# Three products instead of four in a spectral layer, and column terms read from a column-ordered copy

## The chip, the cores and the metric

The kernel runs on one core of a Trainium2 chip. The metric is device time in microseconds (us), the median of several runs. The core has a matrix engine (TensorE, PE in the profile, with its weight loads shown apart as PEld), a vector engine (VectorE, DVE), an activation engine (ScalarE, ACT), GpSimd (POOL) and a queue that issues the transfers (SyncE, SP). Each takes its instructions in order and waits for the others by semaphores. Matrix products are written to PSUM, in eight banks; everything else lies in SBUF.

## The reference

An image of 48 x 48 tokens with 768 channels goes through a transformer block and then through a spectral layer. Shortened to what matters here:

```python
# layer 0: attention with decomposed relative positions, 12 heads of 64 channels
q, k, v = heads(layernorm(x) @ qkv_w + qkv_b)
attn = einsum('bqc,bkc->bqk', q * scale, k)
rel_h = einsum('bhwc,hkc->bhwk', q.reshape(nh, 48, 48, hd), rel_pos_h[coords])
rel_w = einsum('bhwc,wkc->bhwk', q.reshape(nh, 48, 48, hd), rel_pos_w[coords])
attn = softmax(attn + rel_h[..., :, None] + rel_w[..., None, :])
x = x + (attn @ v) @ proj_w + proj_b
x = x + gelu(layernorm(x) @ mlp_w1 + mlp_b1) @ mlp_w2 + mlp_b2
# layer 1: spectral layer, 8 blocks of 96 channels
xr, xi = rfft2(x)
o1r = relu(xr @ w1[0] - xi @ w1[1] + b1[0])
o1i = relu(xi @ w1[0] + xr @ w1[1] + b1[1])
o2r = softshrink(o1r @ w2[0] - o1i @ w2[1] + b2[0], 0.01)
o2i = softshrink(o1i @ w2[0] + o1r @ w2[1] + b2[1], 0.01)
y = irfft2(o2r + 1j * o2i) + x
```

All data are float32. The first spectral layer is a complex product, written with four real products per block of 96 channels.

## The kernel before

**Stages.** The kernel normalises the tokens and makes queries, keys and values (written to DRAM by pairs of heads), then runs attention pair after pair, then the projection, the MLP in three passes over 768 tokens (projection aside, the large products are done by a scheme with seven products of half size in place of eight), and last the spectral layer: a Fourier transform along the rows, written to DRAM and read back by frequency, the work along the columns, and the way back. A general path behind a test on the data is not taken.

**Attention.** There are six pairs of heads (`pr`), six chunks of 384 queries (`c`) and two halves of the 2304 keys (`u`); one *run* is one (pr, c, u), with nine key tiles of 128. A run first makes the nine score tiles. For each, `scores` issues two products q·k (L552) and two that add the position terms (L558) into one of three PSUM buffers `sp`, and ScalarE takes the exponential out of it (L562). VectorE adds the exponentials up (L619). Then come the products of the run before with the values (`products`, L567), in groups, and between the groups small pieces of work. After the second half of a chunk `set_aside` copies the finished output out of PSUM on ScalarE (L575); `finish` sums the denominators (L582), reads them on ScalarE (L587) and divides.

**Position terms.** `columns(pr, i)` makes the column terms of eight image columns: for each column w and each head of the pair one product of 48 queries against 48 positions (L262). The queries lie in `qT` in the order (chunk of 8 image rows, block of 16 image columns, row, column), so the 48 queries of one image column are read from `qT` 16 elements (64 bytes) apart. `relative(pr, c)` does the same for the image rows of one chunk (L284); its 48 queries are three groups of 16 neighbours. Both write into one PSUM bank (`small_bank`, a single one during attention), and `two_parts` takes it out with two ScalarE copies (L233 and L234) and one VectorE subtraction (L235). The terms of pair pr + 1 are made during pair pr: the six `columns` in the runs (3,1), (4,0) and (4,1), two in each, and the first `relative` in (5,0) and (5,1). `fetch` brings the next pair's queries and keys in at run (1,0). For pair 0 this happens in the stage before. The column terms are kept in `col_parts`, from which transfers on the SP queue (L297, L301) build the tiles `terms` that L558 reads.

**Spectral stage.** One `Unit` is a half of the channels (four blocks of 96) and up to four of the 25 kept frequencies; there are 14 units, 12 with four frequencies (192 columns per block) and 2 with one (48 columns). In each round four steps i are taken, and in each step, in this order: `back(i)` of the unit three rounds older (L1240), `second(i)` of the one two rounds older (L1221), `first(i)` of the one a round older (L1197, L1198) and `columns(i)` of the newest (L1178). `first(i)` does all frequencies of block i: four products into one PSUM tile `lp`, then real part with bias and relu on VectorE (L1199), imaginary part on ScalarE (L1203), and the negated imaginary part on GpSimd (L1207), all into `o1`. `second(i)` does all four blocks of frequency i and so needs the outputs of all four `first` of its unit; it uses `o1` as the weights. `balanced_copy` takes `columns` and `back` out of PSUM, on VectorE for even i (L77) and ScalarE for odd i (L75). Rounds near the end also hold pieces of `rows_back` (L1261), the transform back along the rows with the last addition.

**Order.** PE's order is that of the text throughout; SP's is too, up to the end of attention. The other queues are ordered by a scheduler at build time, except where the text says otherwise. Matrix products of float32 appear as two PE instructions (two passes) in the profile.

Of the kernel before, what the change touches and what calls it, by code (L numbers as in the profile page):

```python
# [9 lines left out]
F32 = mybir.dt.float32  # L10
# [34 lines left out]
def block_then_afno(  # L45
# [143 lines left out]
    with ExitStack() as flag_scope:  # L189
# [11 lines left out]
        with ExitStack() as att:  # L201
# [18 lines left out]
            def small_bank():  # L220
                banks.append(banks.pop(0))
                return banks[-1]
# [16 lines left out]
            def fetch_values(pr):  # L239
                nc.sync.dma_start(  # L240
                    out=heads[pr][2], in_=v_d[:, ts(pr, P)].rearrange("(k p) f -> p k f", p=P)
                )

            def fetch(pr, pool=None):
# [7 lines left out]
                nc.sync.dma_start(out=kT, in_=k_d[pr])  # L252
                heads[pr] = qT, kT, v.rearrange("p (k f) -> p k f", k=NT)

            def columns(pr, i):

                qT = heads[pr][0].rearrange("p (c b h w) -> p b w c h", c=6, b=3, h=8)
                ps = small_bank().rearrange("p (w c h) -> p w c h", w=8, h=8)
                for r in range(8):
                    w = 8 * i + r  # L260
                    for j in range(2):
                        nc.tensor.matmul(  # L262
                            ps[ds(64 * j, HW), r], relT[:, j, 1, 47 - w : 95 - w],
                            qT[:, w // 16, w % 16], start=True, stop=True,
                        )
                hi, lo = (
                    a.rearrange("p (c b h w) -> p b w c h", c=6, b=3, h=8)[
                        :, i // 2, ds(8 * (i % 2), 8)
                    ]
                    for a in (col_hi, col_lo)  # L270
                )
                two_parts(hi, lo, ps)
# [260 lines left out]
            with tc.manual_schedule(engines={mybir.EngineType.PE, mybir.EngineType.SP}):  # L533
# [4 lines left out]
                small_banks(psum, 1)  # L538
                kv_b = att.enter_context(tc.tile_pool(name="att_kv_b", bufs=1))
                o_pool = att.enter_context(tc.tile_pool(name="att_o", bufs=2))  # L540
                kv = [None, kv_b]
                exps = main.rearrange("p (n j q) -> p n j q", n=18, j=2)
                RUN = 9

                def scores(pr, c, kt, p):

                    qT, kT = heads[pr][:2]
                    a, b = divmod(kt, 3)
                    sp = psum.tile([P, 2, 512], F32, name="sp", bufs=3)
                    for j in range(2):  # L550
                        at = slice(64 * j, 64 * j + 64)
                        nc.tensor.matmul(  # L552
                            sp[:, j, :G], kT[at, ts(kt, P)], qT[at, ts(c, G)],
                            start=True, stop=False,
                        )
                    for j in range(2):
                        at = slice(64 * j, 64 * j + 64)
                        nc.tensor.matmul(  # L558
                            sp[:, j, :G], select[at, a % 2], ready[pr, c][at, a // 2, b],
                            start=False, stop=True,  # L560
                        )
                    nc.scalar.activation(p, sp[:, :, :G], AF.Exp, scale=HD**-0.5)  # L562

                def products(op, v, kt0, ps, first):
                    for i in range(first, first + 3):
# [35 lines left out]

                runs = [(pr, c, u) for pr in range(NC) for c in range(T // G) for u in range(2)]
                waiting = done = op = acc = None
                for n, (pr, c, u) in enumerate(runs):
                    if (c, u) == (1, 0) and pr < NC - 1:
                        fetch(pr + 1, kv[(pr + 1) % 2])
                    if (c, u) == (2, 0) and pr < NC - 1:
                        fetch_values(pr + 1)
                    if (c, u) == (4, 0) and pr == NC - 1:
                        nc.sync.dma_start(out=pw, in_=proj_w.rearrange("(c p) f -> p c f", p=P))  # L610
                    if u == 0:
                        acc = o_pool.tile([P, 2, G], F32, name="acc")
                    made = []
                    for i in range(RUN):
                        kt = RUN * u + i
                        p = exps[:, (RUN * n + i) % 18]
                        scores(pr, c, kt, p)
                        if kt:
                            nc.vector.tensor_tensor(acc, made[0] if kt == 1 else acc, p, ALU.add)  # L619
                        made.append(p)  # L620
                    small = []
                    if u and c < 3:
                        small.append(partial(relative, pr, c + 3))
                    if pr < NC - 1:
                        if (c, u) in ((3, 1), (4, 0), (4, 1)):
                            i = 2 * (2 * (c - 3) + u - 1)
                            small += [partial(columns, pr + 1, i), partial(columns, pr + 1, i + 1)]
                        if (c, u) == (5, 0):
                            small += [partial(relative, pr + 1, 0), partial(relative, pr + 1, 1)]
                        if (c, u) == (5, 1):  # L630
                            small.append(partial(relative, pr + 1, 2))
                    if u and done:
                        small.insert(1, partial(finish, *done))
                    for i in range(3):
                        if waiting and i:
                            products(*waiting, 3 * (i - 1))
                        if i < len(small):
                            small[i]()
                    if waiting:
                        products(*waiting, 6)  # L640
                        if u == 0:
                            done = (*runs[n - 1][:2], done_acc, set_aside(waiting[0]))
                    if u == 0:
                        op = psum.tile([P, G], F32, name="op")
                    else:
                        done_acc = acc
                    waiting = (op, heads[pr][2], RUN * u, made)
                for i in (0, 3, 6):
                    products(*waiting, i)
                finish(*runs[-1][:2], acc, set_aside(waiting[0]))  # L650
# [457 lines left out]
    with ExitStack() as sp:  # L1108
# [20 lines left out]
        a1 = view(BS, 2, NB, BS)  # L1129
        a2 = view(BS, NB, 2, BS)  # L1130
        d2 = view(2 * HW, NB, BS)
        a1n = view(BS, NB, BS)
        irows = view(4 * KW, 6, P)
        icols = view(2 * HW, 2 * HW)
        cols = view(2 * HW, 2 * HW)
# [9 lines left out]
            )  # L1145
        nc.sync.dma_start(out=icols, in_=c_icols)
        nc.sync.dma_start(out=irows, in_=c_irows)
        nc.vector.tensor_scalar(a1n, a1[:, 1], -1.0, None, ALU.mult)

        z2_h = [z.rearrange("(r k) c -> r k c", k=KW) for z in z2]  # L1150
        NBH = NB // 2
# [4 lines left out]
        class Unit:  # L1156
# [27 lines left out]
            def first(self, i):  # L1184

                if i == 0:

                    self.o1 = mid.tile([BS, NBH, 4, 3, HW], F32, name="o1")
                b = NBH * self.half + i
                re, im = (  # L1190
                    self.xf[:, i, t, : self.nk, :].rearrange("p k h -> p (k h)") for t in range(2)
                )
                lp = psum.tile([BS, 2, 4 * HW], F32, name="lp", tag="l")
                for t, (wr, wi) in enumerate(
                    ((a1[:, 0, b], a1n[:, b]), (a1[:, 1, b], a1[:, 0, b]))
                ):
                    nc.tensor.matmul(lp[:, t, : self.n], wr, re, start=True, stop=False)  # L1197
                    nc.tensor.matmul(lp[:, t, : self.n], wi, im, start=False, stop=True)  # L1198
                nc.vector.tensor_scalar(  # L1199
                    self.o1[:, i, : self.nk, 1], by_k(lp[:, 0, : self.n]), d1[:, 0, b : b + 1], 0.0,  # L1200
                    ALU.add, ALU.max,
                )
                nc.scalar.activation(  # L1203
                    self.o1[:, i, : self.nk, 2], by_k(lp[:, 1, : self.n]), AF.Relu,
                    bias=d1[:, 1, b : b + 1],
                )
                nc.gpsimd.tensor_scalar(  # L1207
                    self.o1[:, i, : self.nk, 0], self.o1[:, i, : self.nk, 2], -1.0, None, ALU.mult
                )
# [22 lines left out]
            def back(self, i):  # L1232

                if i >= self.nk:
                    return
                zz = self.zz[i]
                if i % 2 == 0:
                    self.y = mid.tile([2 * HW, 2, CH], F32, name="y", bufs=3)
                yp = psum.tile([2 * HW, CH], F32, name="yp", tag="y")
                nc.tensor.matmul(  # L1240
                    yp, icols, zz.rearrange("p n o -> p (n o)"), start=True, stop=True
                )
                balanced_copy(i, self.y[:, i % 2, :], yp)
                if i % 2 or i == self.nk - 1:
                    n = i % 2 + 1
                    nc.sync.dma_start(
                        out=z2_h[self.half][:, ds(self.k0 + i + 1 - n, n), :], in_=self.y[:, :n]
                    )
# [169 lines left out]
```

## Time and profile before

The median of 3 runs is 2955.97 us (2951.86 to 2956.34). The profiled execution took 2962.34 us, of which 2960.5 us are the span of its instructions.

| stretch of the profiled execution | us | PE busy | ACT busy | DVE busy | POOL busy |
|---|---|---|---|---|---|
| 533 to 1495, most of attention | 962.0 | 962.0 | 562.4 | 707.8 | 43.0 |
| 1650 to 2696, MLP and rows forward | 1046.0 | 1037.0 | 149.2 | 675.1 | 330.4 |
| 2696 to 2916, the spectral units | 220.0 | 218.8 | 43.3 | 101.7 | 84.8 |
| 2916 to the end, rows back | 44.5 | 35.4 | 0.0 | 14.0 | 0.0 |

Busy times are sums of the stretches in which an engine has an instruction under way. A matrix product is pipelined: the next starts before it ends, so the distance between two starts says more of PE than the duration of one.

### The profile page before, as it was taken

Reading aid. Unit: us, or ns where it says so; the run is one execution under the profiler, and the core shown is the slowest. Engines: PE = TensorE matmul, PEld = TensorE weight load, DVE = VectorE, ACT = ScalarE, POOL = GpSimd, SP = SyncE. Lnnn points to the kernel's source line nnn. Section 1 sums busy time; section 2 is a strip of 40 time slices with the busy share of each in tenths; the row PEclk is TensorE's granted clock in tenths of the full one; section 3 lists DMA queues with packets and bytes.
Section 4 is the critical chain, followed back from the end, with each engine's and each line's share of the span. In section 5 each row is a group of like instructions: output and inputs, shape, how many; then the busy total and the mean of one; then the engine's idle time right before and its main releaser. Section 6 shows DMA issues by size and latency. Waiting matters only on the chain. (4 is left out here: it accounts for less than half of the span.)

```text
span 2960.5 us, 40962 instructions
## 1 busy us (share of the span) xinstructions
PE 2902.6 (98%) x15771; PEld 1762.2 (60%) x15771; DVE 1768.2 (60%) x2548; ACT 881.1 (30%) x1372; POOL 610.2 (21%) x564
## 2 busy tenths in 40 slices
PE   6999999999999999999999999999999999999998
PEld 4555655555556555555555555555555555557995
DVE  4342327777777777777633666675666566665443
ACT  1011125555556555565500210122011211111210
POOL 2302110000000000000043223342332323322441
PEclk9999999999999999999999999999999999999999
DMA  3423275173461725535252111112111211213225
GB/s 119 150 83 123 88 163 123 26 135 64 75 132 33 139 42 97 113 50 89 59 177 75 42 54 54 64 62 68 54 64 60 75 49 64 64 57 93 83 83 174
DMA packets 202817, 253.03 MB, mean 85 GB/s; under 512 B 21618, under 2 KB 180978, under 8 KB 201078
## 3 DMA queue, kind: packets, MB, share of 16 engines
q1 hardware_dynamic: 202614, 250.32, 33.2%
q8 instruction: 127, 2.08, 0.3%
q14 instruction: 76, 0.62, 0.1%
HBM read 136.40 MB, written 50.14 MB: 63 GB/s over the span
## 5 line engine op out<-in xcount | busy, mean ns | idle before, releaser
L619 DVE TENSOR_TENSOR acc<-acc,main 128x768 f32<-128x768 f32 x576 | 551.9, 958 | 202.0 <-ACT main L562 145.4
L562 ACT ACTIVATE main<-sp 128x768 f32<-128x768 f32 x648 | 522.1, 811 | 155.8 <-PE sp L558 148.6
L558 PE MATMUL sp<-terms,select 64*128 64x384 f32 x1296 | 413.1, 630 | 0.0
L1032 DVE TENSOR_TENSOR main<-o,main 128x384 f32<-128x384 f32 x540 | 299.4, 556 | 41.0 <-PE o L1030 2.1
L970 PE MATMUL h<-shared,w 128*128 128x384 f32 x864 | 296.6, 486 | 0.8 <-issue 0.8
L552 PE MATMUL sp<-shared 64*128 64x384 f32 x1296 | 267.9, 490 | 2.2 <-DVE o L452 2.2
L552 PE MATMUL sp<-qT,kT 64*128 64x384 f32 x1296 | 266.5, 487 | 0.0
L597 POOL TENSOR_TENSOR inverse<-inverse,rden 128x384 f32<-128x384 f32 x36 | 46.3, 1287 | 1031.6 <-DVE rden L594 961.6
L441 PE MATMUL m<-main 128*128 128x384 f32 x756 | 248.4, 490 | 6.2 <-DVE main L172 2.9
L970 PEld LDWEIGHTS h<-shared,w 128*128 128x128 f32 x864 | 164.4, 190 | 116.1 <-issue 2.2
L970 PE MATMUL h<-shared,w1s 128*128 128x384 f32 x648 | 226.6, 486 | 0.0
L567 PE MATMUL op<-main,shared 128*64 128x384 f32 x1296 | 221.3, 488 | 0.0
L567 PE MATMUL op<-main,v 128*64 128x384 f32 x1296 | 219.9, 488 | 0.0
L441 PEld LDWEIGHTS m<-main 128*128 128x128 f32 x756 | 143.4, 191 | 108.7 <-issue 10.1
L976 ACT ACTIVATE hT<-c,vec 128x384 f32<-128x384 f32 x108 | 66.4, 615 | 466.1 <-DVE c L982 466.0
L982 DVE TENSOR_TENSOR c<-h,u 128x384 f32<-128x384 f32 x108 | 60.2, 557 | 212.4 <-PE h L970 212.4
L1030 PE MATMUL o<-w,hT 128*128 128x384 f32 x432 | 175.2, 487 | 3.7 <-DVE mv L118 2.0
L1030 PE MATMUL o<-w2s,hs 128*128 128x384 f32 x432 | 174.9, 487 | 1.4 <-DVE hs L155 1.3
L558 PEld LDWEIGHTS sp<-terms,select 64*128 64x128 f32 x1296 | 125.6, 187 | 84.1 <-issue 0.5
L970 PEld LDWEIGHTS h<-shared,w1s 128*128 128x128 f32 x648 | 123.1, 190 | 85.9
L154 POOL TENSOR_TENSOR w1s<-w 128x384 f32<-128x384 f32 x36 | 36.2, 1006 | 612.5 <-PE o L1030 420.8
L552 PEld LDWEIGHTS sp<-shared 64*128 64x128 f32 x1296 | 117.7, 187 | 60.3 <-issue 23.1
(150 smaller groups left out, 3892.3 us busy)
## 6 DMA issues: line engine op xcount, KB each, us to landing
w<-in_mlp_w_dram SPq DMA_DIRECT2D x72, 768.0 KB
terms<-col_parts SPq DMA_DIRECT2D x432, 72.0 KB
terms<-row_hi SPq DMA_DIRECT2D x216, 72.0 KB
terms<-row_lo SPq DMA_DIRECT2D x216, 72.0 KB
main<-in_qkv_w_dram SPq DMA_DIRECT2D x36, 384.0 KB
z<-zt SPq DMA_DIRECT2D x48, 150.0 KB
zo<-z SPq DMA_DIRECT2D x12, 600.0 KB
x<-in_x_dram SPq DMA_DIRECT2D x18, 384.0 KB
```

The source lines that it names most:

```text
L441: nc.tensor.matmul(bank, a[:, c, :], b[:, c, :], start=(first and c == 0), stop=(c == 2), skip_group_check=not first,)
L552: nc.tensor.matmul(sp[:, j, :G], kT[at, ts(kt, P)], qT[at, ts(c, G)], start=True, stop=False,)
L558: nc.tensor.matmul(sp[:, j, :G], select[at, a % 2], ready[pr, c][at, a // 2, b], start=False, stop=True,)
L562: nc.scalar.activation(p, sp[:, :, :G], AF.Exp, scale=HD**-0.5)
L567: nc.tensor.matmul(op[ts(j, 64)], v[:, kt0 + i, ts(j, 64)], ps[i][:, j, :], start=(kt0 + i == 0), stop=(kt0 + i == NT - 1),)
L597: nc.gpsimd.tensor_tensor(inverse, inverse, rden, ALU.add)
L619: nc.vector.tensor_tensor(acc, made[0] if kt == 1 else acc, p, ALU.add)
L970: nc.tensor.matmul(bank[i], a[:, c, :], b[:, c, :], start=(start and c == 0), stop=(c == 2), skip_group_check=not start,)
L976: nc.scalar.activation(h[:, i, ts(k, G)], src, AF.Gelu, bias=col(V_B1 + 2 * n + i))
L982: nc.vector.tensor_tensor(t, src, other, ALU.add)
L1030: nc.tensor.matmul(bank[k], a, b, start=start, stop=True, skip_group_check=not start)
L1032: nc.vector.tensor_tensor(dst, bank[k], dst, ALU.add)
```

## The change

There are three parts.

1. `first(i)` uses three products per block instead of four. With re, im the two parts and w0, w1 the weights, it makes l1 = (re + im)·w0, then re·(w1 - w0) and im·(-w1 - w0); the real part is l1 plus the third, the imaginary part l1 plus the second. VectorE makes re + im (`both`), ScalarE copies l1 out of PSUM (`p_both`), VectorE adds it to both products at once (`pre`), and both relus are done on ScalarE. The PSUM tile l1 has one buffer; the tile `yp` of `back` goes from two buffers to one. Two weight tables `a1d` and `a1e` are made by three VectorE operations in place of one.
2. For the pairs 1 to 5, `columns` reads `by_column`, in which the 48 queries of a column are neighbours. ScalarE makes it with 30 copies of 128 x 384 (`in_columns`), two at the end of each of the runs (2,1), (3,0) and (3,1).
3. During attention ScalarE's order is that of the text.

```diff
@@ columns
+                bank = small_bank()
+                ps = bank.rearrange("p (w c h) -> p w c h", w=8, h=8)
                 for r in range(8):
                     w = 8 * i + r
                     for j in range(2):
                         nc.tensor.matmul(
-                            ps[ds(64 * j, HW), r], relT[:, j, 1, 47 - w : 95 - w],
-                            qT[:, w // 16, w % 16], start=True, stop=True,
+                            bank[ds(64 * j, HW), ts(r, HW)] if pr else ps[ds(64 * j, HW), r],
+                            relT[:, j, 1, 47 - w : 95 - w],
+                            by_column[:, w] if pr else qT[:, w // 16, w % 16],
+                            start=True, stop=True,
                         )
@@ attention
+                by_column = o_pool.tile([P, HW, HW], F32, name="by_column", bufs=1)
...
+                def in_columns(pr, i):
+
+                    q = heads[pr][0].rearrange("p (c b h w) -> p b w c h", c=6, b=3, h=8)
+                    nc.scalar.copy(
+                        by_column[:, ts(i, 8)].rearrange("p w (c h) -> p w c h", c=6),
+                        q[:, i // 2, ds(8 * (i % 2), 8)],
+                    )
...
+                with tc.manual_schedule(engines={mybir.EngineType.Activation}):
                     for n, (pr, c, u) in enumerate(runs):
...
                         if waiting:
                             products(*waiting, 6)
                             if u == 0:
                                 done = (*runs[n - 1][:2], done_acc, set_aside(waiting[0]))
+                        if pr < NC - 1 and (c, u) in ((2, 1), (3, 0), (3, 1)):
+                            for i in range(2):
+                                in_columns(pr + 1, 2 * (2 * (c - 2) + u - 1) + i)
@@ spectral stage
-        a1n = view(BS, NB, BS)
+        a1d = view(BS, NB, BS)
+        a1e = view(BS, NB, BS)
...
-        nc.vector.tensor_scalar(a1n, a1[:, 1], -1.0, None, ALU.mult)
+        nc.vector.tensor_tensor(a1d, a1[:, 1], a1[:, 0], ALU.subtract)
+        nc.vector.tensor_scalar(a1e, a1[:, 1], -1.0, None, ALU.mult)
+        nc.vector.tensor_tensor(a1e, a1e, a1[:, 0], ALU.subtract)
@@ first
+                both = mid.tile([BS, 4 * HW], F32, name="both", bufs=3)
+                nc.vector.tensor_tensor(both[:, : self.n], re, im, ALU.add)
+                l1 = psum.tile([BS, 4 * HW], F32, name="l1", tag="l1", bufs=1)
                 lp = psum.tile([BS, 2, 4 * HW], F32, name="lp", tag="l")
-                for t, (wr, wi) in enumerate(
-                    ((a1[:, 0, b], a1n[:, b]), (a1[:, 1, b], a1[:, 0, b]))
-                ):
-                    nc.tensor.matmul(lp[:, t, : self.n], wr, re, start=True, stop=False)
-                    nc.tensor.matmul(lp[:, t, : self.n], wi, im, start=False, stop=True)
-                nc.vector.tensor_scalar(
-                    self.o1[:, i, : self.nk, 1], by_k(lp[:, 0, : self.n]), d1[:, 0, b : b + 1], 0.0,
-                    ALU.add, ALU.max,
+                nc.tensor.matmul(lp[:, 0, : self.n], a1e[:, b], im, start=True, stop=True)
+                nc.tensor.matmul(lp[:, 1, : self.n], a1d[:, b], re, start=True, stop=True)
+                nc.tensor.matmul(
+                    l1[:, : self.n], a1[:, 0, b], both[:, : self.n], start=True, stop=True
                 )
-                nc.scalar.activation(
-                    self.o1[:, i, : self.nk, 2], by_k(lp[:, 1, : self.n]), AF.Relu,
-                    bias=d1[:, 1, b : b + 1],
+                p = mid.tile([BS, 4 * HW], F32, name="p_both", bufs=3)
+                nc.scalar.copy(p[:, : self.n], l1[:, : self.n])
+                pre = mid.tile([BS, 2, 4 * HW], F32, name="pre", bufs=2)
+                nc.vector.tensor_tensor(
+                    pre[:, :, : self.n], lp[:, :, : self.n],
+                    p[:, : self.n].unsqueeze(1).to_broadcast([BS, 2, self.n]), ALU.add,
                 )
+                for t in range(2):
+                    nc.scalar.activation(
+                        self.o1[:, i, : self.nk, 1 + t], by_k(pre[:, t, : self.n]), AF.Relu,
+                        bias=d1[:, t, b : b + 1],
+                    )
...
-                yp = psum.tile([2 * HW, CH], F32, name="yp", tag="y")
+                yp = psum.tile([2 * HW, CH], F32, name="yp", tag="y", bufs=1)
```

The order of the instructions otherwise: PE, SP and GpSimd issue the same as before but for the products named and the place of four small loads for the spectral weights. On ScalarE the attention part differs by the 30 copies alone, and in the spectral part `xf` of odd steps now stands between the copy of l1 and the two relus of the same step. On VectorE the last `pre` of a round is followed by the first `both` of the next, then the copy of `yp`, then two more `both`.

More of the change, by code (lines that the diff above doesn't have):

```diff
@@ L253, in fetch @@
                 heads[pr] = qT, kT, v.rearrange("p (k f) -> p k f", k=NT)
+            by_column = None
             def columns(pr, i):
                 qT = heads[pr][0].rearrange("p (c b h w) -> p b w c h", c=6, b=3, h=8)
-                ps = small_bank().rearrange("p (w c h) -> p w c h", w=8, h=8)
+                bank = small_bank()
+                ps = bank.rearrange("p (w c h) -> p w c h", w=8, h=8)
                 for r in range(8):
@@ L603, in block_then_afno @@
                 waiting = done = op = acc = None
[L604 to L640, printed above, removed]
-                        if u == 0:
[L642 to L647, printed above, removed]
@@ new lines, in block_then_afno @@
+                with tc.manual_schedule(engines={mybir.EngineType.Activation}):
+                    for n, (pr, c, u) in enumerate(runs):
+                        if (c, u) == (1, 0) and pr < NC - 1:
+                            fetch(pr + 1, kv[(pr + 1) % 2])
+                        if (c, u) == (2, 0) and pr < NC - 1:
+                            fetch_values(pr + 1)
+                        if (c, u) == (4, 0) and pr == NC - 1:
+                            nc.sync.dma_start(out=pw, in_=proj_w.rearrange("(c p) f -> p c f", p=P))
+                        if u == 0:
+                            acc = o_pool.tile([P, 2, G], F32, name="acc")
+                        made = []
+                        for i in range(RUN):
+                            kt = RUN * u + i
+                            p = exps[:, (RUN * n + i) % 18]
+                            scores(pr, c, kt, p)
+                            if kt:
+                                nc.vector.tensor_tensor(acc, made[0] if kt == 1 else acc, p, ALU.add)
+                            made.append(p)
+                        small = []
+                        if u and c < 3:
+                            small.append(partial(relative, pr, c + 3))
+                        if pr < NC - 1:
+                            if (c, u) in ((3, 1), (4, 0), (4, 1)):
+                                i = 2 * (2 * (c - 3) + u - 1)
+                                small += [partial(columns, pr + 1, i), partial(columns, pr + 1, i + 1)]
+                            if (c, u) == (5, 0):
+                                small += [partial(relative, pr + 1, 0), partial(relative, pr + 1, 1)]
+                            if (c, u) == (5, 1):
+                                small.append(partial(relative, pr + 1, 2))
+                        if u and done:
+                            small.insert(1, partial(finish, *done))
+                        for i in range(3):
+                            if waiting and i:
+                                products(*waiting, 3 * (i - 1))
+                            if i < len(small):
+                                small[i]()
+                        if waiting:
+                            products(*waiting, 6)
+                            if u == 0:
+                                done = (*runs[n - 1][:2], done_acc, set_aside(waiting[0]))
+                        if pr < NC - 1 and (c, u) in ((2, 1), (3, 0), (3, 1)):
+                            for i in range(2):
+                                in_columns(pr + 1, 2 * (2 * (c - 2) + u - 1) + i)
+                        if u == 0:
+                            op = psum.tile([P, G], F32, name="op")
+                        else:
+                            done_acc = acc
+                        waiting = (op, heads[pr][2], RUN * u, made)
```

## The prediction

> **What bounds the kernel now.** I read the page first, then the busy time by stretches, then the timeline in the two places that the change touches.
>
> ```profile
> span 2960.5 us, 40962 instructions
> PE 2902.6 (98%) x15771; PEld 1762.2 (60%) x15771; DVE 1768.2 (60%) x2548; ACT 881.1 (30%) x1372; POOL 610.2 (21%) x564
> ```
>
> By stretches (the window, its length, busy time of PE, PEld, DVE, ACT and POOL, the granted clock, the DMA share, GB/s):
>
> ```profile
> 533.00:1495.00 962.00, 962.00 (x7891) 555.75 (x7888) 707.80 (x707) 562.37 (x797) 42.99 (x34) 1.00 0.43 83
> 2696.00:2916.00 220.00, 218.75 (x1798) 195.65 (x1798) 101.73 (x220) 43.26 (x105) 84.83 (x106) 1.00 0.32 94
> ```
>
> TensorE has work in all of attention and in all but 1.3 us of the spectral units. So TensorE time saved there is time saved, until another engine's answer is late. Two questions follow: how much TensorE work goes, and which answer is late next.
>
> The timeline around a block of column terms (L262) and one of row terms (L284):
>
> ```profile
> 1108.47 1.55 PE L262 MATMUL small<-shared,relT 128*48 128x48 f32 x32
> 1109.84 2.12 PE L567 MATMUL op<-main,v 128*64 128x384 f32 x12
> ...
> 1040.99 0.93 PE L284 MATMUL small<-qT,relT 128*48 128x48 f32 x32
> 1041.75 2.12 PE L567 MATMUL op<-main,v 128*64 128x384 f32 x12
> ```
>
> Both blocks are 32 passes over 48 columns with equal weights. From first start to the next group's start the column terms take 1.37 us, the row terms 0.76. What differs is how the moving operand is read: 64 bytes apart, or in runs of 16 neighbours.
>
> ScalarE at the end of run (3,0) of one pair (set_aside, then the next run's exponentials), with the fourth score tile's start:
>
> ```profile
> 883.24 0.48 ACT L575 COPY ot<-op 128x384 f32<-128x384 f32 x1 [5.15 <-PE op L567]
> 884.25 6.55 ACT L562 ACTIVATE main<-sp 128x768 f32<-128x768 f32 x8 [0.54 <-PE sp L558]
> 885.68 0.81 PE L552 MATMUL sp<-shared 64*128 64x384 f32 x4
> ```
>
> Eight exponentials take 6.55 us, 0.82 each, and a score tile also takes 0.82 on TensorE: ScalarE can't catch up within a run. The first exponential ends at 885.07, and the fourth tile, which reuses its buffer, starts at 885.68: some 0.6 us of room.
>
> The end of a unit's last `first` and the start of the next round:
>
> ```profile
> 2736.96 0.49 PE L1198 MATMUL lp<-xf,shared 96*96 96x192 f32 x2
> 2737.28 0.84 PE L1178 MATMUL fp<-shared,zi 96*96 96x96 f32 x8
> 2737.48 0.41 DVE L1199 TENSOR_SCALAR o<-lp,d 96x192 f32<-96x192 f32 x1 [0.29 <-PE lp L1198]
> 2737.93 0.42 ACT L1203 ACTIVATE o<-lp,d 96x192 f32<-96x192 f32 x1 [2.63 <-DVE o L1199]
> 2737.96 0.81 PE L1240 MATMUL yp<-zz,shared 96*96 96x384 f32 x2
> 2738.25 0.46 ACT L75 COPY xf<-fp 96x384 f32<-96x384 f32 x1
> 2738.43 0.69 POOL L1207 TENSOR_SCALAR o<-o 96x192 f32<-96x192 f32 x1 [0.16 <-ACT o L1203]
> 2738.61 1.52 PE L1221 MATMUL mp<-shared,o 96*96 96x96 f32 x16
> ```
>
> This is the one tight loop: product, VectorE, ScalarE, GpSimd, and back to TensorE, which uses the result as weights in `second`. GpSimd ends at 2739.12. The 16 passes of `second` start 0.085 apart; the last block's first pass is the 13th (2739.63), and the pass that needs GpSimd's result is the 15th (2739.80). Between the last `first` and that pass lie the other work of the round, `columns` 0.68 and `back` 0.65. So 0.68 us of room today.
>
> **Column terms, gain.** 30 of the 36 blocks change (pairs 1 to 5). The new operand is fully contiguous, so the row terms' price applies: 30 x (1.37 - 0.76) = 18.3 us. Bounds: nothing, if the reading is not the cause; and some 20, if 48 neighbours go slightly better than three groups of 16.
>
> **Column terms, cost.** ScalarE gets 30 copies. No row shows ScalarE reading SBUF with such a stride. Near rows: PSUM to SBUF without stride 0.48 (L575), the cast that writes `col_parts` in this same stride 0.84. I take 0.84, the row with the like stride, 0.48 as the lower end.
>
> ```profile
> L234 ACT CAST col_parts<-small 128x384 fp32r<-128x384 f32 x36 | 30.0, 833 | 0.0
> L234 ACT CAST row_hi<-small 128x384 fp32r<-128x384 f32 x36 | 17.5, 485 | 0.0
> ```
>
> The Trainium skill, "SBUF — State Buffer", in its note on cachelines under Door 1, says that SBUF has lines of 16 bytes and that each access into a new line pays a penalty. By it both the old products and the new copies pay, which agrees with the 1.37 against 0.76 above; no run here shows a strided read by ScalarE alone, and the page would make me take the upper end, as the L234 rows do. With 0.48 a copy the sum at the end would be 27.6 us, by the page 23.9 or less.
>
> Two copies (1.68) stand at the end of three runs. At (2,1) and (3,1) ScalarE idles 4.28 and 1.72 us before the next exponentials (the timeline at 870.74 and 901.15), which covers them; the queries were asked for at 830.5, three runs earlier. At (3,0) program order puts them behind set_aside, which waits for the last value product, so the 5.15 us of idle time ahead of it does not help: exponentials start at 883.72 + 1.68 = 885.40, the first ends at 886.22, 0.54 after TensorE wants its buffer. ScalarE then stays late through the run, and the single bank of the first column block comes free about 0.2 late for `finish`. 0.74 x 5 pairs = 3.7 us; at 0.48 a copy it is nothing. If the idle cover at (3,1) went too, another 5 x 1 or so.
>
> **Spectral layer, gain.** In the timeline the eight passes of a full `first` start at 2735.98 and `columns` follows at 2737.28: 1.30 us, 0.1625 a pass. Two passes less: 0.325 x 48 = 15.6 us. The eight short ones take 0.64, so 0.16 x 8 = 1.3. Sum 16.9.
>
> **Spectral layer, cost.** Count from the end of the last `first` pass (2737.45 = 0), signals of 0.04 to 0.08 as above. Copy of l1: 0.04 to 0.45 (0.41 as for 96x192 rows). `pre`, 96x384 with PSUM input, 0.55 (L1225): 0.49 to 1.04. In ScalarE's new order xf stands ahead of the relus; `columns` frees it at 0.80, and it ends at 1.26. Two relus of 0.42: 2.10. GpSimd 0.69 from 2.18: 2.87. Needed at 2.35, less some 0.13 for the weight load ahead of it (2738.61 shows PEld one step before PE): 2.22. TensorE waits 0.65 us, once per unit, not per block, since the other three blocks have a round. Eight units are of this kind: 5.2. The first unit has no `back` in between (deadline 0.65 earlier: 1.3), the sixth no `columns` and no xf (1.1). The two short units and the two among the last rounds have 0.45 to 2.0 us of room today and other work in between; I put none on them. Sum 7.6. Lower bound 2: relus overlapping as L233 and L234 do (0.38 from start to start at 0.48) and a copy at 0.30. Upper bound 16.9, GpSimd slowed.
>
> For that last: VectorE's first and second `both` of the next round (two SBUF inputs) fall beside GpSimd's negation, and the rows of L157 show operations of that kind stretching, VectorE from 546 to 1346 ns and GpSimd from 993 to 1322, where both run at once. The same page, under "Who interferes with whom", has a VectorE operation with two SBUF inputs and a GpSimd operation lock each other out whole. It would add at most one `both` (an estimate of 0.35 from the page's rule and the 0.41 row) to ten waits, 3.5 us, and the sum would be 20.4. Without the page the rows of L157 alone put the upper bound there.
>
> **At no cost.** Two more VectorE operations on the weight tables, 0.55 each, fall before 2662, where VectorE idles 3.31 us at 2659.34; without that cover 1.1 us. The single `yp` is copied out within 1.5 us of its product and wanted again after 3.66. VectorE per step goes from about 1.86 to 2.35 of 3.66 us. The four moved loads go out with the same neighbours.
>
> **Sum.** 18.3 - 3.7 + 16.9 - 7.6 = 23.9 us. Against its own execution 2960.5 - 23.9 = 2936.6 of span; that execution (2962.34) stands 6.4 above the median, so 2955.97 - 23.9 = 2932.
>
> **Rivals.**
> - *Spectral gain handed back.* Room 0.68 us, chain longer by 1.2 at least; with GpSimd and xf both late, 1.2 to 1.5 us a unit takes the 16.9. Against: the round has 14.6 us, only its seam is tight. Time 2955.97 - 14.6 = 2941.
> - *Both costs hidden.* Copies at 0.48 and overlapping relus: 18.3 + 16.9 - 2 = 33, time 2923.
> - *The copy changes nothing on TensorE*, the stride not being the cause, so that 1.37 stays. Against: no other difference between the two blocks. 16.9 - 7.6 - 3.7: time 2950.
> - *Slower: ScalarE becomes the bound of attention.* Place: the six copies per pair ahead of exponentials that can't catch up. If one takes d, (3,0) loses 2d - 1.1, (3,1) 2d - 2.3, (2,1) 2d - 4.8. At d = 3 us: 4.9 + 3.7 + 1.2 = 9.8 a pair, 49 in all, against gains of 18.3 + 9.3: time 2977. It decides from about d = 2.5. Against: the strided row is 0.84.
>
> **How the numbers follow.** The forecast as summed, 2925 to 2938: 0.59. Gain handed back (2938 to 2946): 0.18. Both hidden (2918 to 2925): 0.08. Copy without effect (2946 to 2956): 0.09. Slower: 0.06. Time 2932; range 2919 to 2946, which leaves out the last two and the lower edge, 0.17. About 0.2%, 5.9 us, is what a measurement of this kernel can tell from no change. Of the copy-without-effect case 0.03 ends below 2950, the rest within the bound, and so does 0.01 of the handed-back case: faster 0.59 + 0.17 + 0.08 + 0.03 = 0.87, same 0.07, slower 0.06.
>
> **What would show it.** L262 of pairs 1 to 5 at some 0.76 us a block; the copies' mean between 480 and 850 ns; TensorE idle or a wider start distance at the first score tiles of (3,1) and nowhere else in attention; in the spectral units six passes in 0.98 us a step, and in `second` one late pass per round, ended by GpSimd, of about 0.65. The prediction is wrong if L262 stays at 1.37, if ScalarE's copies are beyond 1 us, or if TensorE waits within every step.

## The result, and the profile after

The changed kernel takes 2927.09 us (median of 4 runs, 2923.02 to 2934.48), the kernel before in the same comparison 2955.19: 0.9911 of it, 95% interval 0.9899 to 0.9923, some 28 us less. In a second comparison the ratio was 0.9910 (0.9891 to 0.9929). The forecast was 2932.

The head of the page after:

```profile
span 2922.9 us, 40961 instructions
PE 2864.6 (98%) x15659; PEld 1724.2 (59%) x15659; DVE 1791.0 (61%) x2606; ACT 936.3 (32%) x1514; POOL 609.8 (21%) x564
```

TensorE has 112 instructions less and is as full as before; ScalarE has 55 us more work. The span is 37.6 us shorter than that of the execution before, more than the medians tell. To see why, the profiled executions of the kernels are cut below at the starts of events that each has, read from the timelines: the first score product, the last product with the values, the first product of the first spectral layer, the last of the second layer, and the end of the span.

| us | before | after | spectral only | columns only | no program order | copies early | relus swapped | repaired |
|---|---|---|---|---|---|---|---|---|
| up to attention | 431.8 | 425.9 | 432.7 | 427.2 | 427.1 | 426.6 | 429.3 | 429.6 |
| attention | 1062.5 | 1045.6 | 1062.5 | 1045.6 | 1057.7 | 1043.7 | 1045.7 | 1043.8 |
| projection, MLP, rows forward | 1206.2 | 1204.4 | 1205.4 | 1207.0 | 1205.2 | 1205.7 | 1203.2 | 1203.6 |
| spectral units | 208.8 | 198.6 | 198.6 | 208.8 | 198.6 | 198.6 | 193.9 | 192.8 |
| rest | 51.2 | 48.3 | 50.0 | 50.0 | 49.0 | 50.8 | 47.1 | 53.0 |
| span | 2960.5 | 2922.9 | 2949.2 | 2938.6 | 2937.6 | 2925.4 | 2919.2 | 2922.8 |

Attention and the spectral units repeat to 0.05 us in kernels that share that part. The first, third and fifth row vary by 4 to 7 us between kernels that are the same there, or differ there only by the weight tables and one wait, both under 1 us (see below); the rest is the spread of the runs. So the change is worth 16.9 us in attention and 10.2 in the spectral units; what the two spans differ in beyond these 27.1 lies in the rows that vary.

**Attention after.** The end of run (3,0) in the timeline, as shown of before, and the first column block:

```profile
870.53 0.48 ACT L590 COPY ot<-op 128x384 f32<-128x384 f32 x1 [5.15 <-PE op L582]
870.90 1.59 ACT L574 COPY by_column<-qT 128x384 f32<-128x384 f32 x2
872.39 6.91 ACT L569 ACTIVATE main<-sp 128x768 f32<-128x768 f32 x9
873.26 0.30 PEld L559 LDWEIGHTS sp<-shared 64*128 64x128 f32 x4 [0.59 <-ACT main L569]
...
878.38 0.93 PE L265 MATMUL small<-by_column,relT 128*48 128x48 f32 x32
879.14 1.15 PE L582 MATMUL op<-main,shared 128*64 128x384 f32 x6
```

The block takes 0.76 us from start to start, where it took 1.37. The two copies stand between set_aside and the exponentials, and the fourth score tile waits for the first exponential. That score phase takes 7.97 us where all others after the first take 7.58: 0.39 us, in each of five pairs, and nothing else in attention is later.

**The spectral seam after.** From the last `first` of a unit to the second layer of the next round:

```profile
2710.11 0.49 PE L1223 MATMUL l<-both,shared 96*96 96x192 f32 x2
2710.44 0.84 PE L1202 MATMUL fp<-shared,zi 96*96 96x96 f32 x8
2710.64 0.32 ACT L1227 COPY p_both<-l 96x192 f32<-96x192 f32 x1 [1.56 <-PE l L1223]
2710.99 0.55 DVE L1229 TENSOR_TENSOR pre<-lp,p_both 96x384 f32<-96x384 f32 x1 [0.31 <-ACT p_both L1227]
2711.32 0.47 ACT L75 COPY xf<-fp 96x384 f32<-96x384 f32 x1 [0.36 <-PE fp L1202]
2711.69 0.80 ACT L1234 ACTIVATE o<-pre,d 96x192 f32<-96x192 f32 x2
2711.76 1.35 PE L1252 MATMUL mp<-shared,o 96*96 96x96 f32 x14
...
2712.57 0.76 DVE L1218 TENSOR_TENSOR both<-xf 96x192 f32<-96x192 f32 x2
2712.58 0.88 POOL L1238 TENSOR_SCALAR o<-o 96x192 f32<-96x192 f32 x1 [0.82 <-ACT o L1234]
2713.51 0.41 PE L1252 MATMUL mp<-shared,o 96*96 96x96 f32 x2 [0.40 <-POOL o L1238]
```

Read it as a chain: l1, copy, addition, xf, two relus, negation, and TensorE stops after the 14th pass of `second` until GpSimd is done. From the 14th start (2712.87) to the 15th (2713.51) it is 0.64 us instead of 0.085. GpSimd's negation takes 0.88 where it took 0.69, beside two `both` on VectorE. The loss of such a unit, counted over the 15th and the 16th start against steps of 0.085, is 0.64 as well. The first unit loses 1.1 us in all and the sixth 1.0, as they lack other work in the round; all the waits of the second layer come to 7.0 us (0.2 in the kernel before).

### The profile page after: what moved, and what is told of

Its sections match the earlier page's. It is cut to its first block, busy times and chain, and to the rows that moved or that the text cites. A ratio compares the mean times of both kernels' runs of the same rounds, so it can differ in the third digit from the quotient of the medians.

```text
span 2922.9 us, 40961 instructions
## 1 busy us (share of the span) xinstructions
PE 2864.6 (98%) x15659; PEld 1724.2 (59%) x15659; DVE 1791.0 (61%) x2606; ACT 936.3 (32%) x1514; POOL 609.8 (21%) x564
```

## The experiments

**Each part by itself.** Two kernels: the kernel before with one part of the diff each.

```diff
 (spectral only: the kernel before up to the spectral stage, the changed one from there)
-        a1n = view(BS, NB, BS)
+        a1d = view(BS, NB, BS)
+        a1e = view(BS, NB, BS)
...
```

> The kernel before with the spectral part of the change alone (three products, one yp buffer, two weight tables). Theory (each part is worth its TensorE time less the waits it makes): from the first product of the first layer to the last product of the second some 10.2 us shorter than before, as in the changed kernel, with one wait of 0.64 us per unit in the second layer; attention unchanged at 7.58 us of scores per run and 1.35 us per column block; the whole about 9 to 11 us below before. Rival (the parts help each other, or what the changed kernel gained outside attention and the spectral stage belongs to this part): clearly more than 12 or less than 7 us.

Measured: 2941.19 us against 2955.35, ratio 0.9952 (0.9938 to 0.9966); units 198.6 us as in the changed kernel, attention 1062.5 as before, waits of 0.64 per unit. The median moved 14 us, beyond the 12 allowed, so the times alone do not refute the rival: their interval reaches from 10 to 18 us. The trace does for this stage, where the part is worth 10.2, as in the changed kernel.

```diff
 (columns only: the changed kernel up to the spectral stage, the kernel before from there)
+                by_column = o_pool.tile([P, HW, HW], F32, name="by_column", bufs=1)
...
+                            in_columns(pr + 1, 2 * (2 * (c - 2) + u - 1) + i)
...
```

> The kernel before with the column part alone (copies on ScalarE, contiguous reads, ScalarE in program order during attention). Theory: attention 16.9 us shorter (5 x 3.76 less 5 x 0.39), spectral stage as before; the whole about 15 to 19 us below before. Rival (a good part of the 28 us came from something that neither part owns, such as the transfers before attention): below 13 or above 22 us.

Measured: 2938.95, ratio 0.9942 (0.9925 to 0.9959); attention 1045.6, units 208.8. In the traces the parts are independent: each stage is as long as in the changed kernel, 27.1 us less in the two together. The medians of the parts add to 30.6 us, the whole is 28.1 below before, which is the same within the spread.

**Is the program order on ScalarE needed?** The same changed kernel, without it:

```diff
-                with tc.manual_schedule(engines={mybir.EngineType.Activation}):
-                    for n, (pr, c, u) in enumerate(runs):
+                for n, (pr, c, u) in enumerate(runs):
```

> The changed kernel without the fixed program order on ScalarE: the scheduler now places the six copies of a pair in one run, between exponentials. Theory (ScalarE keeps no more than TensorE's pace in the score phase, 0.82 us a tile for both, so a copy among exponentials is paid beyond some 0.6 us of buffer room): six copies of 0.85 are 5.1 us, so one score phase per pair grows from 7.58 to about 12 us; five pairs lose 20 to 23 us, which takes the whole column gain and leaves the kernel at 2945 to 2952 us. Rival (the fixed order is only a matter of form, the copies hide wherever they stand): within 3 us of the changed kernel.

Measured: 2940.63, ratio 0.9947 (0.9931 to 0.9964), and attention at 1057.7. ScalarE's timeline in one pair:

```profile
683.51 3.25 ACT L569 ACTIVATE main<-sp 128x768 f32<-128x768 f32 x4 [4.28 <-PE sp L565]
686.65 2.37 ACT L574 COPY by_column<-shared 128x384 f32<-128x384 f32 x3
688.90 0.83 ACT L569 ACTIVATE main<-sp 128x768 f32<-128x768 f32 x1
689.61 1.63 ACT L574 COPY by_column<-shared 128x384 f32<-128x384 f32 x2
691.11 0.84 ACT L569 ACTIVATE main<-sp 128x768 f32<-128x768 f32 x1
691.81 0.88 ACT L574 COPY by_column<-shared 128x384 f32<-128x384 f32 x1
692.56 2.23 ACT L569 ACTIVATE main<-sp 128x768 f32<-128x768 f32 x3
```

All six copies stand among the exponentials of one score phase. That phase takes 10.65 us instead of 7.58 in three pairs and 11.47 in a fourth. In the remaining pair the copies begin after the sixth exponential instead of the fourth, TensorE finishes its score tiles into the three buffers, and the phase stays at 7.58. The clock tells the fourth pair from the three: around its copies the mean clock is 0.72, in the same place of another pair 1.00 (the last three figures of a row are clock, DMA share and GB/s).

```profile
690.00:696.00 6.00, 4.88 (x32) 2.15 (x32) 4.04 (x5) 4.79 (x7) 0.00 (x0) 1.00 0.75 120
1047.00:1053.00 6.00, 4.88 (x21) 2.12 (x22) 3.83 (x4) 3.92 (x6) 0.00 (x0) 0.72 0.71 123
```

Against the changed kernel attention loses 12.1 us. The sign was as expected; the loss is half of the 20 to 23 us, and the kernel is faster than the 2945 to 2952 that were forecast. Three things make it smaller. Nine exponentials without copies take 7.35 us and these end after 11.28, so six copies add 3.9 us and not 5.1, since each begins before the one ahead of it has ended; with the room in the buffers TensorE loses 3.1 a pair. One pair of five loses nothing. And the 0.39 of run (3,0) is gone in all five pairs, 1.95 us. About 1.6 us of the 12.1 goes with the low clock in the fourth pair (its run is 18.25 us long, those of the three others 16.6). The rival falls: with 12.1 of 16.9 us, most of the column gain hangs on where the copies stand.

**What makes a column block slow?** The products read the queries at a distance of 1, 2, 3, 4 and 16 elements, one distance per pair:

```diff
-                            by_column[:, w] if pr else qT[:, w // 16, w % 16],
+                            heads[pr][0][:, bass.DynSlice(8 * w, HW, step=STEP[pr])] if pr
+                            else qT[:, w // 16, w % 16],
```

> The changed kernel, but the column products of pair 1, 2, 3, 4, 5 read 48 elements of the queries at a distance of 1, 2, 3, 4, 16 elements (4, 8, 12, 16, 64 bytes) instead of the column-ordered copy; the copies are still made, and the column terms are not the reference's. Theory (the distance between elements sets the time of a pass): a block of 32 passes takes about 0.74 us at distance 1 and 1.35 at 16. By lines of 16 bytes with two hits per line enough, 2 elements would be as fast as 1, and 4 as slow as 16. Rival (the column blocks were slow for another reason, such as a new operand tile or the four-dimensional pattern): all five alike, near 0.74.

A block and the group that follows it, at the distances 2, 3, 4 and 16:

```profile
703.59 0.93 PE L266 MATMUL small<-shared,relT 128*48 128x48 f32 x32
704.35 0.51 PE L584 MATMUL op<-main,v 128*64 128x384 f32 x2
...
878.99 1.27 PE L266 MATMUL small<-qT,relT 128*48 128x48 f32 x32
880.09 0.50 PE L584 MATMUL op<-main,shared 128*64 128x384 f32 x2
...
1056.41 1.61 PE L266 MATMUL small<-shared,relT 128*48 128x48 f32 x32
1057.83 0.52 PE L584 MATMUL op<-main,v 128*64 128x384 f32 x2
...
1235.85 1.53 PE L266 MATMUL small<-qT,relT 128*48 128x48 f32 x32
1237.20 0.50 PE L584 MATMUL op<-main,shared 128*64 128x384 f32 x2
```

From start to start: 0.76, 1.10, 1.42, 1.35 us; at distance 1 it is 0.76. So the reading distance is the cause: at 16 elements, in a pattern of one plain step, the block takes 1.35 us, as the old reading did. A distance of two elements is free, three cost 1.45 times, four as much as sixteen. The Trainium skill says in "SBUF — State Buffer", in the note on cachelines under Door 1, that SBUF has lines of 16 bytes and needs at least two accesses to each for full rate: the times at 2, 3, 4 and 16 elements agree with that. The same note puts the distance that one can stride for free at 4 float32 elements; here 3 and 4 elements are not free, and the measurement decides.

**The waits, one by one.** First the copies of (3,0) ahead of the value products:

```diff
+                        if pr < NC - 1 and (c, u) == (3, 0):
+                            for i in range(2):
+                                in_columns(pr + 1, 2 + i)
                         small = []
...
-                        if pr < NC - 1 and (c, u) in ((2, 1), (3, 0), (3, 1)):
+                        if pr < NC - 1 and (c, u) in ((2, 1), (3, 1)):
```

> The changed kernel with the two copies of run (3,0) issued ahead of the value products and set_aside instead of behind them, into ScalarE's 5 us of idle time. Theory (program order behind set_aside is what makes the first score tiles of (3,1) wait): that score phase goes from 7.97 to 7.58 us in each of five pairs, attention is 1.9 to 2.0 us shorter than in the changed kernel, nothing else moves. Rival (the copies as such cost, by slowing ScalarE or the reads of others): it stays at 7.97 or the wait shows up at another run.

```profile
865.13 1.60 ACT L574 COPY by_column<-qT 128x384 f32<-128x384 f32 x2
870.39 0.48 ACT L590 COPY ot<-op 128x384 f32<-128x384 f32 x1 [3.65 <-PE op L582]
871.40 7.37 ACT L569 ACTIVATE main<-sp 128x768 f32<-128x768 f32 x9 [0.54 <-PE sp L565]
```

ScalarE now copies in time that it had idle, and the exponentials again wait for TensorE. All score phases take 7.58, attention 1043.7: 1.95 us less, as expected. Its one time was 2927.41 us; the difference is too small for the whole time.

Then the imaginary relu first:

```diff
-                for t in range(2):
+                for t in (1, 0):
                     nc.scalar.activation(
                         self.o1[:, i, : self.nk, 1 + t], by_k(pre[:, t, : self.n]), AF.Relu,
```

> The changed kernel with the imaginary relu ahead of the real one, so that GpSimd can start a relu earlier (0.35 to 0.4 us). Theory (the chain product, copy, addition, relu, relu, negation sets the wait in the second layer): the wait per unit goes from 0.64 to 0.2 to 0.3 us and GpSimd still ends it; ten such waits, some 3.5 us in all. Rival (GpSimd is held by the two additions re + im on VectorE, which stand at the same place in time whatever ScalarE does): GpSimd starts earlier, but ends at the same time, and the wait stays above 0.5.

```profile
2713.09 0.80 ACT L1234 ACTIVATE o<-pre,d 96x192 f32<-96x192 f32 x2
2713.16 1.62 PE L1252 MATMUL mp<-shared,o 96*96 96x96 f32 x16
...
2713.63 0.69 POOL L1238 TENSOR_SCALAR o<-o 96x192 f32<-96x192 f32 x1 [0.48 <-ACT o L1234]
2713.96 0.61 DVE L1218 TENSOR_TENSOR both<-xf 96x192 f32<-96x192 f32 x2
```

The wait between units is gone, not just 0.35 shorter: GpSimd starts 0.35 earlier (0.54 us behind the start of the first relu instead of 0.89), ahead of the two `both`, and takes its 0.69 again. Units 193.9 us, 4.75 less than in the changed kernel; the first and the sixth still wait. Both the length of the chain and the neighbour on VectorE were in the 0.64. The changed kernel itself has one unit that shows the second alone: there GpSimd starts at 2824.61, 0.15 ahead of the two `both`, takes 0.68, and TensorE loses 0.44 instead of 0.64. The one time of the kernel with swapped relus was 2921.19 us.

**All repairs together,** with the weight tables on GpSimd and l1 first of the three products, beside the changed kernel again:

```diff
-        nc.vector.tensor_tensor(a1d, a1[:, 1], a1[:, 0], ALU.subtract)
+        nc.gpsimd.tensor_tensor(a1d, a1[:, 1], a1[:, 0], ALU.subtract)
...
+                nc.tensor.matmul(
+                    l1[:, : self.n], a1[:, 0, b], both[:, : self.n], start=True, stop=True
+                )
+                nc.scalar.copy(p[:, : self.n], l1[:, : self.n])
                 nc.tensor.matmul(lp[:, 0, : self.n], a1e[:, b], im, start=True, stop=True)
                 nc.tensor.matmul(lp[:, 1, : self.n], a1d[:, b], re, start=True, stop=True)
...
```

> The changed kernel with four repairs: copies of (3,0) ahead of the value products; the shared product l1 first of the three, so that its copy lies beside the other two; the imaginary relu first; the weight tables made on GpSimd instead of VectorE. Theory (the three waits found are all that the change gives back): attention 1.95 us shorter, spectral units 6.5 to 6.9 us shorter with no wait in the second layer, 0.6 us in the MLP; some 9 us below the changed kernel, 2917 to 2920 beside 2927. Rival (some of these waits cover others, so that taking them away uncovers the next): less than 5 us.

> The changed kernel itself, on the same chip as the repaired one, for the comparison. Every theory: 2923 to 2934 us, 0.990 to 0.992 of before; the waits in the second layer 0.64 us per unit again.

Measured: repaired 2920.77 (2914.34 to 2924.57, ratio to before 0.987, 0.9847 to 0.9894), changed 2929.89 (2926.21 to 2932.14). 9.1 us between the medians, where 9 were expected; the four and five runs do not overlap, though the intervals of the ratios touch. In the trace: attention 1.9 less; units 5.8 less, below the 6.5 to 6.9 expected, since the first and the sixth unit still wait (1.2 us together); and 0.4 is lost ahead of them, as TensorE waits 0.95 instead of 0.56 us before the first layer for `both`, which its first product now needs. With the tables' wait, 0.6 in the changed kernel's own trace here, that is 7.9 us. The rest of the 9.1 no trace shows, so that they came to the expected 9 is in part luck. It is the fastest of the kernels run with several rounds.

```profile
2711.35 0.80 ACT L1237 ACTIVATE o<-pre,d 96x192 f32<-96x192 f32 x2 [0.99 <-DVE pre L1232]
2711.81 1.52 PE L1255 MATMUL mp<-shared,o 96*96 96x96 f32 x16
2711.89 0.69 POOL L1241 TENSOR_SCALAR o<-o 96x192 f32<-96x192 f32 x1
```

The relus now start 0.46 ahead of `second`, and its 16 passes run through.

## Why the prediction was right, by its steps

- **What bounds the kernel.** TensorE in both stages, shown: each part alone shortens its own stage, by the same amount as in the whole.
- **Column terms, gain.** Forecast 18.3 us, measured 18.8. The three runs with column blocks are 1.25 us shorter each per pair (16.88 to 15.64 and the like from one first score product to the next, with the copies early and so without their wait), 0.625 a block against 0.61. The cause, reading at 64 bytes, is shown by the distances.
- **Column terms, cost.** Forecast 3.7 us, measured 1.95, the one mis-sized term of attention. Place and mechanism were right. The copy was priced well:

```profile
L574 ACT COPY by_column<-qT 128x384 f32<-128x384 f32 x18 | 14.4, 854 | 0.0
L574 ACT COPY by_column<-shared 128x384 f32<-128x384 f32 x12 | 9.6, 849 | 0.0
```

  Too large were two things. Two copies in a row take 1.59 and the exponential begins 0.10 before the last ends, where the forecast set ends to starts: 0.39 instead of 0.54. And the 0.2 for the bank at `finish` does not exist: its weight load waits 0.18 (0.17 in the kernel before), and the value products around it go on without a gap.
- **Program order.** The forecast used its order and did not price it. Without it the column part is worth 12 us less.
- **Spectral gain.** Forecast 16.9 us. Without the waits of the second layer (7.0, 2.2 and 1.2 us in the changed kernel, the one with swapped relus and the repaired one, 0.2 before) the units are 16.9 to 17.0 us shorter in all three kernels.
- **Spectral cost.** Forecast 7.6 us, measured 7.0, of which 0.2 was there before: seven waits of 0.64, one of 0.44 (the unit above where GpSimd starts ahead of the two `both`), 1.1 in the first unit and 1.0 in the sixth. The forecast had 0.65, 1.3 and 1.1. That 0.65 came so close is luck, since inside it two errors cancel: the copy xf ends 0.07 earlier than summed, the relus begin 0.10 before its end and take 0.80 for both, not 0.84, which takes 0.2 off, and GpSimd's 0.88 puts 0.19 on. The forecast left that stretching to its range; the swapped relus show that it was in the main term.
- **At no cost: the tables.** Wrong, by 0.8 us. They were placed before 2662 in idle time, at 0.55 each. The two additions of tables take 0.94 each, and VectorE runs one of them between the additions that free TensorE's banks, so that four passes that take 1.30 us just before last 2.09 (2628.62 to 2630.71):

```profile
2627.55 0.56 DVE L1171 TENSOR_SCALAR shared<-shared 96x768 f32<-96x768 f32 x1
2628.02 0.55 DVE L1051 TENSOR_TENSOR main<-o,main 128x384 f32<-128x384 f32 x1
2628.49 0.94 DVE L1172 TENSOR_TENSOR shared<-shared 96x768 f32<-96x768 f32 x1
...
2628.62 0.91 PE L1049 MATMUL o<-w2s,hT 128*128 128x384 f32 x2
2629.96 0.91 PE L1049 MATMUL o<-w,hs 128*128 128x384 f32 x2 [0.42 <-DVE main L1051]
2630.71 1.78 PE L989 MATMUL h<-shared,w 128*128 128x384 f32 x5
```

- **The sum.** 23.9 forecast; 18.8 - 1.95 + 10.2 - 0.8 = 26.3 from the traces (10.2 is the spectral gain less its cost); 28.1 between the medians. The interval of the ratio, 22.8 to 29.8, holds all three.
- **The rivals.** Handed back: refuted, the chain costs 6.8 of 17 us. Both hidden: refuted, both waits are there. Copy without effect: refuted by the distances. ScalarE as the bound: the mechanism exists, as the run without program order shows, where one phase in each of four pairs is bound by it; the copy's 0.85 is far below the 2.5 that the rival put as its condition.

## What to carry to other kernels

On an engine that is always full, work taken away is worth its start-to-start distance, and the loss sits at the few seams where a chain through other engines must return within a round: add up that chain against the work in between, in the order that each queue really has. A copy that makes a matrix operand contiguous pays where the old reading was slowed by its distance (here from three float32 elements on), and pays most if it stands in the copying engine's idle time: here its place decided over 12 of 17 us. Where the last engine of such a chain runs beside a VectorE operation with two SBUF inputs, see whether it can start ahead of that: here 0.35 us earlier took away a wait of 0.64.

## What was not expected of the hardware

- Reading every second element (8 bytes apart) costs TensorE nothing, every third 1.10 / 0.76 = 1.45 times, every fourth (1.42 us) slightly more than every sixteenth (1.35).
- GpSimd's negation of 96x192 takes 0.69 us alone and 0.88 when it starts 0.01 us after a VectorE operation with two SBUF inputs (seven units of the changed kernel). When it starts 0.33 us first, in the kernel with swapped relus, it keeps 0.69, and the two VectorE operations that start within it take 0.61 for both, as little as anywhere.
- TensorE's clock is halved for a stretch now and then after a wait. In the kernel after, TensorE waits 2.2 us ahead of attention, and a score tile that takes 0.82 us later in the run then takes 1.53 (426.82 to 428.35). The stretch (its length, then the busy times, the clock, the DMA share, GB/s):

```profile
425.90:435.00 9.10, 9.07 (x54) 6.76 (x56) 4.92 (x6) 7.38 (x9) 0.00 (x0) 0.81 0.64 115
```

  9.10 x 0.19 = 1.7 us lost, by estimate. Which waits are followed by one differs: without program order four pairs have the same waits of 1.1 to 1.4 us, and only one of them got the lower clock. How much of what varies in the rows of the table such stretches explain was not tried.
